# Values and keys of two tiles as seven block products, the norm's last sum on GpSimd, pages turned in place, and the second batch's pages fetched in front

## The chip, the cores and the metric

The kernel runs on one core of a Trainium2 chip. A core has five engines that work side by side, each with its own in-order queue of instructions: TensorE (PE in the profile; its weight loads are shown as PEld), VectorE (DVE), ScalarE (ACT), GpSimd (POOL) and SyncE (SP), which here does nothing but issue transfers. Sixteen DMA engines move data between HBM and the core's memory SBUF; TensorE writes to the small memory PSUM. An instruction waits on semaphores for what it needs, and everything behind it in the same queue waits too.

The metric is device time in microseconds (us) of one launch, as the median over several runs. A profiled execution is one more run, with every instruction recorded.

## What is computed

Sixty-four sequences of 32 rows by 512 columns go through four stages, each added to its input. Everything is in fp32. Cut to what matters:

```python
x = x + einsum('bct,bcd->bdt', x, W0[cond])             # stage 0: mix 32 rows
x = x + x @ base_w.T + bias + (x @ A.T) @ B.T            # stage 1: linear + LoRA
q, k, v = x @ Wq.T, x @ Wk.T, x @ Wv.T                   # stage 2: 32 query heads, 8 kv heads, D = 128
q, k = rope(rmsnorm(q, wq), pos), rope(rmsnorm(k, wk), pos)
k_all = concat(k_cache[block_table], k)                  # 16 pages of 32 keys, then 32 new ones
v_all = concat(v_cache[block_table], v)
probs = softmax(where(valid, q @ k_all.T * SCALE, -1e30))
x = x + (probs @ v_all) @ Wo.T
x = x + einsum('bct,bcd->bdt', x, W3[cond])              # stage 3: mix 32 rows
```

The norm is `t * rsqrt(mean(t*t) + eps) * w` over the 128 columns of a head. The rotation adds two products: the head times the cosines, and its halves exchanged times the sines.

## The kernel before

The 2048 rows are 16 tiles of 128 rows (four sequences each). Stages 0 and 1 run tile by tile (class `First`) at the front of the program and are also laid into the beginning of the attention. The attention dominates. It runs over two groups of 4 kv heads and, in each, over the 16 tiles: 32 steps. A step has four sequences, so there are 128 units, and each unit has four slots, one per kv head: 512 slots in all. One slot's scores are 128 queries (4 heads by 32 rows) against 512 cached and 32 new keys.

The order of instructions on the five engines is written by hand. A table `plan` holds, for each slot, lists of calls under names such as "fetch", "pe", "dve", "act" and "store"; `slot(i)` emits them: transfers, GpSimd's gathers, the scores of this slot (L827, L830), the transposes of an earlier one (L869), pieces of projection, pieces of the norm, head transposes (L745), the values of a still earlier one (L882), then VectorE's softmax (L835, L851, L853), takes of projections, and copies by ScalarE. `home` is the slot from which the offsets of a part are counted, and `begin` is the first slot, 43 before the first scores.

**Projections.** The steps go in pairs of tiles, 16 pairs, with a window of 32 slots each. The projections of a pair lie in the window ahead of its use. Values and keys of the two tiles are four `Plain` products: each is four matmuls over 128 of the 512 input columns (L579), into a PSUM tile `proj_ps` of 128 by 512 that has a single buffer, and ScalarE copies the result out (L589 values, L596 keys). Queries come as two `Block`s. A `Block` computes the two tiles' products with two head columns as one 2 by 2 block product with seven products instead of eight (Strassen's scheme in Winograd's form): seven products of two matmuls each (L646) of sums of x (`x_12`, `x_34`, stored by L514 and loaded by L562) and sums of weights (`block_sum`, L615); ScalarE takes the first, and VectorE adds the others into `raw` (L658).

**Norm.** A norm's squares are summed by ScalarE (L696, one instruction per head). VectorE scales the sum (L701), GpSimd raises it to the power -1/2 (L703, `rstd`), and VectorE does four pieces: `scale` (L708), `straight` (L715), `swapped` (L727, two instructions) and `sum` (L737). TensorE then turns the heads (L745) and ScalarE copies them out (L757). The pieces stand in a list, and each slot takes some if VectorE has few takes in it. There are 160 norms: four of queries and one of keys for each of 32 steps.

**Pages.** The cached keys are turned before use: 16 tiles of 4 pages per group. A page tile is loaded into `page_rows` (L253), turned by TensorE (L269), copied by ScalarE into a second tile `page_T` (L279), and stored to a scratch tensor (L289), beside a plain copy of the values (L285). In front there are four buffers of `page_rows` and two of `page_T`; for the second group there is one of each. Each unit then fetches its 16 pages of keys one by one from the scratch by page number (L783, `kT`, two buffers), in the first slot of the unit before it. The cached values come by gathers on GpSimd (L105, `v_sb`), and the mask of valid keys is `pen` (L798, GpSimd).

**Queues.** Nearly all other transfers are issued by SP, in the order of the program: x (L392), its store (L507), the turned x (L510), the sums (L514), rotary tables (L384), the pages, the pairs' loads (L562, L567), the new values (stored at L592, loaded by L805), `kT`, and the attention's output (L918). Weights of the second group and of the output, and the first outputs read back (L1110), are issued by GpSimd.

**Last stage.** The output projection and the second mix run pair by pair, also with seven products (L1293). For the first pair the weight sums `w_2`, `w_1`, `w_4` are built by VectorE (L1288) after the additions into `x3` (L1303), which wait for loads of x (L1337).

Of the kernel before, what the change touches and what calls it, by code (L numbers as in the profile page):

```python
# [51 lines left out]
NG = 2  # L52
# [25 lines left out]
def resid_kernel(  # L78
# [39 lines left out]
    ints_sb = const.tile([P, N_INT], I32, name="ints_sb")  # L118
    nc.sync.dma_start(out=ints_sb, in_=ints)
# [3 lines left out]


    same = const.tile([P, P], F32, name="same")
    nc.gpsimd.memset(same, 0.0)
    for j in range(NB):
        nc.gpsimd.memset(same[j * S : (j + 1) * S, j * S : (j + 1) * S], 1.0)
# [13 lines left out]
    def rows_of(pool, name, source, n, size, lanes, times=1.0, first=0.0, tag=None):  # L142

        i = pool.tile([P, n], I32, name=name, tag=tag or name)
        for c in range(0, n, 64):
            m = min(n - c, 64)
            f = small.tile([P, 64], F32, name=f"{name}_f", tag="rows_f", bufs=2)
            nc.vector.tensor_scalar(
                f[:, :m], source[:, c : c + m], float(size), lanes, ALU.mult, ALU.add
            )  # L150
            nc.vector.tensor_scalar(i[:, c : c + m], f[:, :m], times, first, ALU.mult, ALU.add)
        return i
# [4 lines left out]
    table = ints_sb[:, I_TABLE : I_TABLE + B * NC]  # L157
# [5 lines left out]
    def channel_diagonal(pool, table, t):  # L163
# [61 lines left out]
    with ExitStack() as l2:  # L225
# [20 lines left out]
        class Turn:  # L246


            def __init__(self, g, c, pool, bufs):
                self.g, self.c, self.pool, self.bufs = g, c, pool, bufs  # L250
                self.first = 2 * g * PAGES * PSIZE + c * P
                self.rows = pool.tile([P, 2, 2 * D], F32, name="page_rows", bufs=bufs[0])
# [22 lines left out]
            def keep(self):  # L275
                self.turned = self.pool.tile(
                    [P, 4, KG, PSIZE], F32, name="page_T", bufs=self.bufs[1]
# [108 lines left out]
        class First:  # L386


            def __init__(self, t):
                self.t = t  # L390
                self.x = first_pool.tile([P, HID], F32, name="x_sb", bufs=5)
# [13 lines left out]
            def diagonal(self):  # L405

                self.diag = first_pool.tile([P, NB, S], F32, name="mix_diag", bufs=2)
# [74 lines left out]
            def keep_out(self):  # L482
                p, i = divmod(self.t, 2)
                pool = first_pool if p else proj_pool
# [3 lines left out]
                if p == 0:  # L488
# [30 lines left out]
        def own_ranks(i):  # L519


            mask_i = first_pool.tile([P, P], I32, name=f"mask_i{i}")
# [3 lines left out]
            low = small.tile([P, P], F32, name="mask_low", bufs=1)  # L526
# [13 lines left out]
        class Pair:  # L540
# [13 lines left out]
            def load(self, name):  # L554
                src = {
                    "a": xT_dram[2 * self.p],
                    "b": xT_dram[2 * self.p + 1],
# [3 lines left out]
                self.x[name] = proj_pool.tile([P, NC, P], F32, name=f"x_{name}")  # L561
# [7 lines left out]
        class Plain:  # L569


            def __init__(self, pair, i, kind):
                self.pair, self.i, self.kind = pair_of[pair], i, kind
                self.step = self.pair.steps[i]

            def project(self, c):
                if c == 0:
                    self.ps = ps_m.tile([P, HID], F32, name="proj_ps", tag="m")
                nc.tensor.matmul(  # L579
                    self.ps,  # L580
                    lhsT=self.pair.x["ab"[self.i]][:, c, :],
                    rhs=w_sb[self.kind][:, c, :],
                    start=(c == 0),
                    stop=(c == NC - 1),
                )

            def take_values(self):
                self.v = proj_pool.tile([P, KG * D], F32, name="v_rows")
                nc.scalar.copy(self.v, self.ps)  # L589

            def store_values(self):
                nc.sync.dma_start(out=vn_dram[self.step.g][self.step.t], in_=self.v)  # L592

            def take_keys(self, norm):
                norm.raw = proj_pool.tile([P, REP, D], F32, name="raw", bufs=6)
                nc.scalar.copy(norm.raw, self.ps.rearrange("p (h d) -> p h d", h=REP))  # L596

        def block_sum(b, what):


            if (what, b) == (3, 0):
                for i, tag in ((2, 7), (1, 6), (4, 8)):
                    w_sb["sum", i] = None
            if what != 3 and w_sb["sum", what] is None:
                w_sb["sum", what] = wpool.tile(
                    [P, 2, NC // 2, REP * D], F32, name=f"sum{what}", tag=f"w{ {1: 6, 2: 7, 4: 8}[what]}"
                )
# [9 lines left out]
        def blocks(b):  # L617
            even, odd = w_sb["q", 2 * b], w_sb["q", 2 * b + 1]
            found = {"11": even[:, lo], "21": even[:, hi], "3": odd[:, lo], "22": odd[:, hi]}
            for i in (1, 2, 4):  # L620
                if w_sb["sum", i] is not None:
                    found[str(i)] = w_sb["sum", i][:, b]
            return found

        class Block:

# [15 lines left out]
            def project(self, i, c):  # L642
                x, half, w = self.ORDER[i]
                if c == 0:
# [3 lines left out]
                    lhsT=self.pair.x[x][:, half][:, c, :],  # L648
# [36 lines left out]

        class Norm:
# [5 lines left out]
            def squares(self):  # L692
                self.ss = small.tile([P, REP], F32, name="ss")
                sq = proj_pool.tile([P, REP, D], F32, name="sq", tag="sq", bufs=2)
                for h in range(REP):
                    nc.scalar.activation(  # L696
                        sq[:, h, :], self.raw[:, h, :], AF.Square, accum_out=self.ss[:, h : h + 1]
# [24 lines left out]
            def swapped(self):  # L722
                which = 3 if self.k is None else 1
                self.b = proj_pool.tile([P, REP, D], F32, name="rot_b", tag="sq", bufs=2)
# [11 lines left out]
            def sum(self):  # L736
                nc.vector.tensor_tensor(self.a, self.a, self.b, ALU.add)  # L737
# [24 lines left out]
        class Unit:  # L762


            def __init__(self, u):
# [7 lines left out]
                at = I_TABLE + b * NC  # L773
                for i in range(NPP // NC):
                    _, page = nc.values_load_multi_w_load_instructions(
                        ints_sb[i * S : i * S + 1, at : at + NC],
# [25 lines left out]
            def fetch_new(self):  # L802

                self.v_new = room["v"].tile([P, D], F32, name="v_new", bufs=3)
# [50 lines left out]
            def flip_new(self):  # L855
# [7 lines left out]
                self.pT_new = room["attn"].tile([P, P], F32, name="pT_new")  # L863
# [75 lines left out]
        def norm_piece(slot):  # L939
# [7 lines left out]
            if norm:  # L947
                slot += 1
# [519 lines left out]
```

## Time and profile before

| what | value |
|---|---|
| median of 3 runs | 2531.39 us (2530.64 to 2532.98) |
| the profiled execution | 2528.74 us |
| its span, first to last instruction | 2526.8 us |
| TensorE matmul busy | 2477.7 us, 98% |
| VectorE busy | 1659.7 us, 66% |
| ScalarE busy | 1281.1 us, 51% |
| GpSimd busy | 1098.3 us, 43% |
| `Plain` matmuls (L579), share of the chain | 9% |
| norm's last sum (L737) | 160 x 717 ns = 114.7 us of VectorE |
| gathers of values (L105) | 512 x 1025 ns = 525.0 us of GpSimd |

In the profile, `L646 PE MATMUL proj_ps<-sum,x 128x512` reads: line 646, engine, operation, what is written and what is read by the program's names, and the shape; `x224` is the number of instructions, and a fp32 matmul counts as two. Behind a bar stand the group's busy time in us, the mean ns of one, and the engine's idle time ahead of the group with what ended it. In an order of time, a line is the start in us, the duration in us, the engine and the instruction, and in square brackets the idle time before and its releaser. The chain of waits is followed back from the last instruction: a "DMA" piece is a transfer under way, an "SPq" piece an issue on SP's queue, an "issue" piece a time in which nothing shown was waited for.

### The profile page before, as it was taken

What the parts mean: (1) busy time and instruction counts of PE and PEld (TensorE: products, weight loads), DVE (VectorE), ACT (ScalarE), POOL (GpSimd) and SP (SyncE); (2) the same over time, 40 slices, a digit from 0 to 9 for tenths busy, and PEclk for the clock granted to TensorE, in tenths of its full rate; (3) what the DMA queues carried; (4) which work ended last, traced back from release to release, by engine and by line L of the source; (5) the groups of instructions that cost most, each with busy time, mean ns of one, the idle gap of its engine ahead of it and who ended that gap; (6) DMA issues with size and microseconds to landing.
All of it is one profiled execution on the core that took longest, in us unless ns stands there. A gap on an engine that the chain in (4) does not pass through costs nothing.

```text
span 2526.8 us, 46803 instructions
## 1 busy us (share of the span) xinstructions
PE 2477.7 (98%) x13824; PEld 1872.2 (74%) x13824; DVE 1659.7 (66%) x4154; ACT 1281.1 (51%) x3671; POOL 1098.3 (43%) x921
## 2 busy tenths in 40 slices
PE   7998999999999999999999999999999999999999
PEld 4555777777777777777777777777777777888887
DVE  5556767677767676787777776777776765433222
ACT  1335666666666666666666666666666644000000
POOL 4325545554545455654545455554555652000000
PEclk9999999999999999999999999999999999999999
DMA  6966666666666667866565656665656774233221
GB/s 225 308 211 195 183 194 190 192 188 191 193 183 196 192 203 216 262 182 195 174 193 164 192 171 181 174 187 167 186 174 214 234 258 157 101 111 127 98 84 59
DMA packets 442556, 461.50 MB, mean 183 GB/s; under 512 B 50560, under 2 KB 364800, under 8 KB 434496
## 3 DMA queue, kind: packets, MB, share of 16 engines
q1 hardware_dynamic: 393200, 296.21, 37.9%
q0 software_dynamic: 49104, 162.31, 21.2%
q8 instruction: 112, 1.84, 0.3%
q14 instruction: 140, 1.15, 0.1%
HBM read 387.02 MB, written 79.69 MB: 185 GB/s over the span
## 4 chain that ended last, share of the span: by engine, by line
PE 91%; DMA 3%; DVE 2%; issue 1%; SPq 1%; ACT 1%; POOL 1%; DVEq 0%; ACTq 0%; POOLq 0%
PE o_ps L882 17%; PE proj_ps L646 14%; PE out_ps L1293 14%; PE s_ps L827 10%; PE proj_ps L579 9%; PE s_ps L830 8%; PE pT_ps L869 8%; PE head_ps L745 3%; PE l_ps L471 2%; PE o_ps L894 2%; DMA kT<-kT 1%; DMA v_sb<-v,v_rows 1%; DMA v_new<-vn 1%; DVE rot_a L737 1%; PE mix_ps L1311 1%
## 5 line engine op out<-in xcount | busy, mean ns | idle before, releaser
L105 POOL DMA_INDIRECT v_sb<-v,v_rows x512 | 525.0, 1025 | 458.4 <-PE o_ps L882 358.7
L835 DVE CUSTOM_DVE_ANT_0 sm<-s_ps,pen 128x544 f32<-128x544 f32 x512 | 370.8, 724 | 453.0 <-PE s_ps L830 447.4
L882 PEld LDWEIGHTS o_ps<-pT,v_sb 128*128 128x128 f32 x4096 | 520.8, 192 | 141.0 <-issue 134.5
L846 ACT ACTIVATE sm<-sm,top 128x544 f32<-128x544 f32 x512 | 382.5, 747 | 460.1 <-DVE top L835 460.0
L882 PE MATMUL o_ps<-pT,v_sb 128*128 128x128 f32 x4096 | 542.2, 275 | 4.1 <-DMA v_sb<-v,v_rows 4.0
L852 ACT ACTIVATE sm<-sm,share 128x512 f32<-128x512 f32 x512 | 369.9, 722 | 181.1 <-DVE share L851 178.1
L703 POOL TENSOR_TENSOR rstd<-ss,minus_half 128x4 f32<-128x4 f32 x160 | 191.8, 1199 | 469.1 <-DVE ss L701 464.2
L827 PE MATMUL s_ps<-kT,qT 128*128 128x288 f32 x1024 | 348.1, 422 | 7.1 <-DMA kT<-kT 4.4
L871 DVE COPY pT<-pT_ps 128x512 f32<-128x512 f32 x512 | 351.1, 686 | 1.6 <-PE pT_ps L869 1.5
L869 PE MATMUL pT_ps<-ident,sm 128*128 128x128 f32 x2048 | 307.7, 273 | 0.0
L830 PE MATMUL s_ps<-kT,qT 128*128 128x256 f32 x1024 | 305.1, 380 | 1.7 <-issue 1.7
L869 PEld LDWEIGHTS pT_ps<-ident,sm 128*128 128x128 f32 x2048 | 256.3, 141 | 51.5 <-issue 0.2
L798 POOL TENSOR_SCALAR pen<-key_f,seq_f 128x544 f32<-128x544 f32 x128 | 279.6, 2184 | 15.9 <-DMA x_b<-xT 5.1
L830 PEld LDWEIGHTS s_ps<-kT,qT 128*128 128x128 f32 x1024 | 194.8, 190 | 56.1 <-issue 2.1
L696 ACT ACTIVATE sq<-raw 128x128 f32<-128x128 f32 x640 | 189.9, 298 | 35.4 <-DVE raw L658 32.0
L105 POOL DMA_INDIRECT mix_rows<-in_w,cond_rows x32 | 34.5, 1077 | 324.2 <-DVE mix_diag L168 307.6
L1342 ACT COPY p<-out_ps 128x256 f32<-128x256 f32 x7 | 2.6, 372 | 340.2 <-PE out_ps L1293 340.2
L1293 PE MATMUL out_ps<-w,o_in 128*128 128x256 f32 x768 | 170.0, 384 | 4.1 <-DVE w L1288 4.1
L827 PEld LDWEIGHTS s_ps<-kT,qT 128*128 128x128 f32 x1024 | 155.1, 191 | 24.3 <-issue 5.0
L1293 PEld LDWEIGHTS out_ps<-w,o_in 128*128 128x128 f32 x768 | 147.8, 193 | 25.1 <-DVE w L1288 4.5
L853 DVE TENSOR_SCALAR p_new<-sm,share 128x32 f32<-128x32 f32 x512 | 148.5, 290 | 18.2
L1293 PE MATMUL out_ps<-wo,o_in 128*128 128x256 f32 x704 | 155.6, 379 | 0.8 <-ACT oT L911 0.8
(160 smaller groups left out, 3442.7 us busy)
## 6 DMA issues: line engine op xcount, KB each, us to landing
kT<-kT SPq DMA_DIRECT2D x2048, 64.0 KB
o<-oT SPq DMA_DIRECT2D x29, 1024.0 KB
o_in<-o SPq DMA_DIRECT2D x28, 1024.0 KB
rot<-rot SPq DMA_DIRECT2D x48, 256.0 KB
page_rows<-in_kv_cache SPq DMA_DIRECT2D x32, 256.0 KB
vn<-v_rows SPq DMA_DIRECT2D x32, 256.0 KB
v<-in_kv_cache SPq DMA_DIRECT2D x32, 256.0 KB
kT<-page_T SPq DMA_DIRECT2D x32, 256.0 KB
```

The lines of the kernel that those rows point to most:

```text
L105: nc.gpsimd.indirect_dma_start(out=dst, out_offset=None, in_=table, in_offset=bass.IndirectOffsetOnAxis(ap=index, axis=0),)
L646: nc.tensor.matmul(self.ps, lhsT=self.pair.x[x][:, half][:, c, :], rhs=blocks(self.b)[w][:, c, :], start=(c == 0), stop=(c == 1),)
L798: nc.gpsimd.tensor_scalar(self.pen, key_f, seq_f[:, self.b : self.b + 1], BIG, ALU.is_ge, ALU.mult)
L827: nc.tensor.matmul(ps[:, first:HID], lhsT=q, rhs=self.kT[:, :n1, k, :], start=True, stop=True)
L830: nc.tensor.matmul(ps[:, HID : first + LA], lhsT=q, rhs=self.kT[:, n1:, k, :], start=True, stop=True)
L835: nc.vector.tensor_tensor_reduce(out=sm, in0=ps[:, first : first + LA], in1=self.pen, scale=1.0, scalar=3e38, op0=ALU.add, op1=ALU.min, ac ...
L846: nc.scalar.activation(sm, sm, AF.Exp, bias=top, scale=-1.0, accum_out=total)
L852: nc.scalar.activation(sm[:, :L], sm[:, :L], AF.Copy, scale=share)
L869: nc.tensor.transpose(ps[:, c, :], self.sm[k][:, c * P : (c + 1) * P], ident)
L871: nc.vector.tensor_copy(pT, ps)
L882: nc.tensor.matmul(self.o_ps[k], lhsT=self.v[c][:, k * D : (k + 1) * D], rhs=self.pT[k][:, c, :], start=(c == 0), stop=False,)
L1293: nc.tensor.matmul(ps[:, :HALF], lhsT=o[:, i, :], rhs=w[i // REP][:, i % REP, :], start=(i == 0), stop=(i == KG * REP - 1),)
```

## The change

1. `Plain` is gone. Values and keys of a pair's two tiles are one more `Block`, `KV`, with seven products of two matmuls. Its even weights are the values', its odd ones the keys', and its weight sums have tiles of their own, built by four more additions per group. ScalarE takes the first product and VectorE the other six. The values are stored from `raw`. Of `x_b` only the half that a `Block` reads is loaded, for the first pair too. The weights of values and keys are loaded earlier in front, and their sums are built there. The slots of the query products move by up to one.
2. The norm's last `sum` is issued on GpSimd as soon as `swapped` is issued on VectorE; the turn of the heads comes at least two slots later, not one. The squares of the heads of a norm are written to one tile of one head's size.
3. Pages are turned in place: ScalarE's copy goes back to `page_rows`. In front the load comes two slots ahead, not three; the second group has one buffer.
4. x tiles have four buffers, not five, and are loaded three slots ahead of `home`, not five. The 16 key pages of unit 1 are fetched in slot -4, not 0.
5. The second group's weights and the output's weights are loaded at other slots. The first pair's early products in the last stage are kept in the weight pool, `w_2` is combined ahead of the additions into `x3`, and the pattern `same` is built anew for the last stage. Integer tables are split into two tiles, and `v_new` and `pT_new` have a buffer less each.

The diff, cut to its core:

```diff
@@ class Turn
-                self.rows = pool.tile([P, 2, 2 * D], F32, name="page_rows", bufs=bufs[0])
+                self.rows = pool.tile([P, 2, 2 * D], F32, name="page_rows", bufs=bufs)
...
-                self.turned = self.pool.tile(
-                    [P, 4, KG, PSIZE], F32, name="page_T", bufs=self.bufs[1]
+                self.turned = self.rows.rearrange("d i f -> d (i f)").rearrange(
+                    "d (p k s) -> d p k s", p=4, k=KG
                 )
@@ class First
-                self.x = first_pool.tile([P, HID], F32, name="x_sb", bufs=5)
+
+            def load(self):
+                t = self.t
+                self.x = first_pool.tile([P, HID], F32, name="x_sb", bufs=4)
                 nc.sync.dma_start(out=self.x, in_=x[t * P : (t + 1) * P, :])
@@ class Pair
-                    "b": xT_dram[2 * self.p + 1],
+                    "b": xT_dram[2 * self.p + 1][:, hi],
@@ def blocks(b)
-            even, odd = w_sb["q", 2 * b], w_sb["q", 2 * b + 1]
+            even, odd = (w_sb[1], w_sb[0]) if b == KV else (w_sb["q", 2 * b], w_sb["q", 2 * b + 1])
@@ class Block
+            def store_values(self, norm, i):
+                step = self.pair.steps[i]
+                nc.sync.dma_start(
+                    out=vn_dram[step.g][step.t], in_=norm.raw.rearrange("p h d -> p (h d)")
+                )
@@ class Norm
-                sq = proj_pool.tile([P, REP, D], F32, name="sq", tag="sq", bufs=2)
+                sq = proj_pool.tile([P, D], F32, name="sq")
...
-                nc.vector.tensor_tensor(self.a, self.a, self.b, ALU.add)
+                nc.gpsimd.tensor_tensor(self.a, self.a, self.b, ALU.add)
@@ def norm_piece(slot)
             piece()
             if norm:
-                slot += 1
+                norm.sum()
+                slot += 2
                 while slot in turning or (slot - VLAG) % KG == KG - 1:
                     slot += 1
@@ def begin_block(pair, b, slots)
-                    norm = Norm(pair, i // 5, 2 * b + (i in (4, 5)))
-                    at(last, "pe", begin_norm, last, norm)
+                    if b != KV:
+                        norm = Norm(pair, i // 5, 2 * b + (i in (4, 5)))
+                    else:
+                        norm = Norm(pair, i // 5)
+                    if b == KV and i in (1, 6):
+                        at(last, "store", block.store_values, norm, i // 5)
+                    else:
+                        at(last, "pe", begin_norm, last, norm)
@@ the plan of the pairs
-            for kind, j, slots in (
-                (1, 0, (0, 0, 1, 2)),
-                (1, 1, (3, 3, 4, 5)),
-                (0, 0, (6, 6, 7, 8)),
-                (0, 1, (9, 9, 10, 10)),
-            ):
...
-                    (11, 11, 12, 13, 14, 14, 15, 16, 17, 17, 18, 19, 20, 20),
-                    (21, 22, 23, 23, 24, 25, 26, 26, 27, 28, 29, 29, 30, 31),
+            for b, slots in (
+                (KV, (0, 0, 1, 2, 3, 3, 4, 5, 6, 6, 7, 8, 9, 9)),
+                (0, (10, 11, 12, 12, 13, 14, 15, 15, 16, 17, 18, 18, 19, 20)),
+                (1, (21, 21, 22, 23, 24, 24, 25, 26, 27, 27, 28, 29, 30, 30)),
...
+                for w, what in zip((-1, 0, 2, 5) if g == 0 else (-12, -11, -10, -9), (3, 2, 1, 4)):
+                    at(home + w, "dve", block_sum, KV, what)
...
-                places = [6, 11, 21, 23, 32, 34] + ([27, 25] if g == NG - 1 else [36, 38])
+                places = (6, 11, 16, 21, 29, 34, 31, 27) if g == NG - 1 else (3, 9, 14, 21, 25, 32)
@@ the plan of the tiles, pages and units
-            at(home - 5 if t > 1 else begin, "fetch", make, *f, First, t)
+            at(home - 3 if t > 1 else begin, "fetch", call, *f, "load")
...
-            at(home - 6, "fetch", lambda t: make(turn_of, t, Turn, 1, t, room["pages"], (1, 1)), t)
+            at(home - 6, "fetch", lambda t: make(turn_of, t, Turn, 1, t, room["pages"], 1), t)
...
-            at(home - 3 if c > 3 else begin + 8, "fetch", make, turn_of, key, Turn, 0, c, start_pool, (4, 2))
+            at(home - 2 if c > 3 else begin + 8, "fetch", make, turn_of, key, Turn, 0, c, start_pool, 4)
...
-            at(KG * (u - 1) if u else ready, "fetch", make, unit_of, u, Unit, u)
+            at(KG * (u - 1) if u > 1 else ready + 2 * u, "fetch", make, unit_of, u, Unit, u)
@@ the program's front
-                at(begin + 6, "store", load_kv_weights, 0, 1, j)
-                at(begin + 8, "store", load_kv_weights, 0, 0, j)
+                at(begin + 3, "store", load_kv_weights, 0, 1, j)
+                at(begin + 4, "store", load_kv_weights, 0, 0, j)
@@ the last stage, first pair
                     p1 = early["p1"]
+                    w_1, w_2, w_4 = new_block("w_1"), new_block("w_2"), new_block("w_4")
+                    combine(w_2, w_3, w11, ALU.add)
                 for at_last in waiting:
                     mixed(*at_last)
...
-                    w_1, w_2, w_4 = new_block("w_1"), new_block("w_2"), new_block("w_4")
-                    combine(w_2, w_3, w11, ALU.add)
```

## The prediction

> **What bounds the kernel now.** I read the page's busy shares and chain first, then windows of the span, then groups of instructions and the order of time at the places that the diff touches. From the page:
>
> ```profile
> PE 2477.7 (98%) x13824; PEld 1872.2 (74%) x13824; DVE 1659.7 (66%) x4154; ACT 1281.1 (51%) x3671; POOL 1098.3 (43%) x921
> ...
> PE 91%; DMA 3%; DVE 2%; issue 1%; SPq 1%; ACT 1%; POOL 1%; DVEq 0%; ACTq 0%; POOLq 0%
> ...
> L835 DVE CUSTOM_DVE_ANT_0 sm<-s_ps,pen 128x544 f32<-128x544 f32 x512 | 370.8, 724 | 453.0 <-PE s_ps L830 447.4
> ```
>
> TensorE is the bound. The last line shows VectorE's slack: once in most of the 512 slots it waits for the scores, 447.4 us / 437 waits = 1.02 us each. Windows (PE, PEld, DVE, ACT, POOL, clock, DMA share, GB/s) show where TensorE is not alone:
>
> ```profile
> 60.00:90.00 30.00, 26.83 (x111) 15.23 (x109) 15.46 (x38) 5.95 (x12) 8.59 (x7) 1.00 0.91 307
> ...
> 400.00:1000.00 600.00, 599.64 (x3555) 447.85 (x3554) 438.34 (x1156) 383.59 (x1106) 309.87 (x251) 1.00 0.66 194
> ...
> 2000.00:2200.00 200.00, 188.39 (x1117) 160.77 (x1116) 124.66 (x271) 75.75 (x188) 71.43 (x67) 0.97 0.58 188
> ```
>
> In the steady part work taken from TensorE should come off one for one. Around 60 to 150 us the DMA is nearly full; at the ends there are stalls.
>
> **Matmuls removed.** Values and keys of a pair of tiles were 4 x 4 matmuls, and become 7 x 2: two fewer for each of 16 pairs. Their price, from the order of time in the steady part:
>
> ```profile
> 1003.19 1.88 PE L646 MATMUL proj_ps<-sum,x_b 128*128 128x512 f32 x4
> ...
> 1007.15 1.02 PE L646 MATMUL proj_ps<-wq,x_a 128*128 128x512 f32 x2
> ...
> 1008.02 1.05 PE L882 MATMUL o_ps<-pT,v_sb 128*128 128x128 f32 x8
> ```
>
> One matmul is two instructions, and from 1007.15 to the next work at 1008.02 it holds TensorE 0.87 us (the four from 1003.19 to 1004.91 give 0.86 each). 30 x 0.86 = 25.8 us for the 15 pairs in the steady part; 1.7 us for the first pair, which stands in the front part and may be covered (0 to 1.7; I take 1). Together -26.8.
>
> **Takes, sums and the norm's last sum.** The groups:
>
> ```profile
> L658 DVE TENSOR_TENSOR raw<-proj_ps,raw 128x512 f32<-128x512 f32 x224 | 150.4, 683 | 7.0 <-PE proj_ps L646 7.0
> ...
> L737 DVE TENSOR_TENSOR rot_a<-rot_a,rot_b 128x512 f32<-128x512 f32 x160 | 114.7, 717 | 0.1
> ...
> L429 POOL TENSOR_TENSOR x_sb<-x_sb,bias_sb 128x512 f32<-128x512 f32 x16 | 20.3, 1270 | 26.8 <-PE x1T_ps L434 21.5 <-DVE v_rows_f L148 4.7 <-PE h_ps L455 0.5
> ```
>
> VectorE gains 7 more accumulating takes per pair (112 x 0.683 = 76.5 us) and 8 weight sums (1.22 us each by the row at 77.97 us in the front part: 9.8), and loses 160 x 0.717 = 114.7: 28 us lighter. ScalarE loses 4 copies and gains 1 per pair: 48 x 0.578 (the copy of L589) = 28 us lighter. GpSimd gains 160 sums. The nearest row is L429's sum of the same shape, 1.27 us: 203 us, 1098 + 203 = 1301 of 2527. None of the three becomes the bound; 64 us more in 600 puts GpSimd at about 62%.
>
> What can leak onto TensorE: (a) the single projection bank: each product's first matmul waits for the take before. In before the waits on VectorE's takes come to 0.5 + 2.3 + 1.5 = 4.3 us for 32 blocks, 0.13 each; 16 more give 2 us, from which ScalarE's takes go (1.2 + 3.7 us, most of that once, in the front part). (b) GpSimd works in order: a sum waits for VectorE's `swapped`, and the gathers of values, the mask `pen` and the next `power` stand behind it. (c) A sum on GpSimd can hold VectorE. Both are seen in the front part:
>
> ```profile
> 76.81 1.28 POOL L429 TENSOR_TENSOR x_sb<-x_sb,bias_sb 128x512 f32<-128x512 f32 x1
> ...
> 83.01 1.27 POOL L429 TENSOR_TENSOR x_sb<-x_sb,bias_sb 128x512 f32<-128x512 f32 x1 [3.00 <-PE x1T_ps L434]
> ```
>
> ```profile
> 77.36 0.69 DVE L426 TENSOR_TENSOR x_sb<-mix_ps,x_sb 128x512 f32<-128x512 f32 x1 [0.57 <-PE mix_ps L417]
> ...
> 83.15 1.27 DVE L373 TENSOR_TENSOR rot<-trig,q_cos 128x128 f32<-128x128 f32 x1 [2.96 <-DMA rot<-rot]
> 84.35 0.28 DVE L373 TENSOR_TENSOR rot<-trig,q_sin 128x128 f32<-128x128 f32 x1
> ```
>
> Beside the sum of 83.01 an SBUF-only 0.28 us operation takes 1.27 and ends with it; beside that of 76.81 an operation with one input in PSUM keeps its 0.69. In a slot the sum follows the slot's last piece; what VectorE does next is L835, the copy of pT and the takes, all reading PSUM, and its 1.02 us pause. So I take little: 0.02 us per sum, 3 us for (b) and (c), 2 for (a) less 1; bounds 0 and 160 x (1.27 - 1.02) = 40 us, the block beyond the mean slack. Steady leak +4. The turn of a head comes a slot later and is due slots ahead: 0.
>
> The Trainium skill ("GPSIMD Engine Reference", section 3.1 Elementwise and section 4.1 Engine selection) speaks against this move: an elementwise operation with two inputs goes to VectorE, GpSimd taking 1.96 times as long; this trace's rows give 1270 / 717 = 1.77. By the page 160 x 0.717 x 1.96 = 225 us on GpSimd, an estimate, in place of 203; either fits beside TensorE, so the sum is the same by both.
>
> **Pages turned in place (front part).** The copy goes back into the page's own buffer; ScalarE no longer waits for the store of two pages before, but the load of page c+4, on SP, waits for the store of page c, issued just ahead of it. Today (order of time, the chain):
>
> ```profile
> 84.39 4.93 DMA kT<-page_T
> ...
> 90.55 3.23 PE proj_ps L579 x4
> ```
>
> Behind the first lies TensorE's one long stall of 60 to 150 us, 3.7 us before 90.55: it goes. In its place SP stands for about 4.9 us (stores there land after 4.1 to 6.6) in each of slots -25 to -14, and behind it are queued the x loads, whose SP wait on the store of x is already 31.6 us in 11 times. By adding up SP's issues and waits I get a two-slot cycle of 10.8 to 13.4 us against TensorE's 10.7: 0 to 2.6 us for 6 cycles, 0 to 15. Loads are issued about 9 us ahead of use and eat part of it: I take +4, less 3.7 = 0 (bounds -3.7 to +12). The x loads two slots before use instead of four share this bound. The half-size x_b load, and the earlier KV weights at 15 to 30 us where TensorE idles anyway, count 0 (0 to 3: 1 MB at 360 GB/s).
>
> **The next keys fetched in front.** The 16 page loads of unit 1 move from slot 0 to slot -4, past x of pair 1, its sums' stores and x_b on SP:
>
> ```profile
> 180.51 9.39 SPq L783 DMA_DIRECT2D kT<-kT  x16
> ...
> 192.64 1.15 SPq L514 DMA_DIRECT2D xS<-x  x2
> 193.89 0.42 SPq L562 DMA_DIRECT2D x_b<-xT  x1
> 198.85 0.65 SPq L805 DMA_DIRECT2D v_new<-vn  x1
> 200.51 10.98 SPq L783 DMA_DIRECT2D kT<-kT  x16
> ```
>
> ```profile
> 199.15 2.12 POOL L798 TENSOR_SCALAR pen<-key_f,seq_f 128x544 f32<-128x544 f32 x1 [5.13 <-DMA x_b<-xT]
> ...
> 208.81 4.03 DMA v_sb<-v,v_rows
> ```
>
> Today the chain runs from the xS store (lands 198.5) over the first mask, the gathers, a second mask, to the values at 212.89, then 1.72 us for unit 1's last keys at 213.93. Afterwards the last of these goes (-1.7), and xS and x_b are issued up to 9.4 us later, unless that queue is early; one or two sums of 1.27 us stand among the gathers. 9.4 + 1.3 - 1.7 = +9; bounds -1.7 and +11; I take +7, as part of those 9.4 us is TensorE work still to do.
>
> **The last stage.** `w_2` is combined ahead of the x3 additions. Today VectorE waits for x there, and TensorE with it:
>
> ```profile
> 2142.31 2.96 DMA x<-x
> ...
> 2145.89 1.15 DVE w L1288
> ```
>
> TensorE is ready at 2143.0 and starts at 2147.08, 4.07 us on L1288. The new order needs only the weights and the space: -4 (bounds -4.1, 0). Other weights' places, 2 or 3 slots earlier or later on GpSimd's queue: 0, within the 6 us that TensorE idles in 2030 to 2065 (bounds -3, +3).
>
> **Sum:** -26.8 + 4 + 0 + 7 - 4 = -19.8. The profiled execution took 2528.74 us (span 2526.8), 2.65 below the median 2531.39 of the runs (2530.64 to 2532.98). 2528.74 - 19.8 = 2509; the median would be 2512, which I predict. Own range: 2502 to 2523.
>
> **Rivals.**
> 1. Everything added is hidden: -26.8 - 4 - 3.7 - 1.7 = -36, at the median 2495 to 2502. For it: slack on three engines. Against: SP's order at 180 to 200 us is a queue, not an average.
> 2. The front part eats the gain: +12 and +11 in place of 0 and +7, and no gain at L1288: -26.8 + 4 + 12 + 11 = 0, 2526 to 2536. For it: DMA at 0.91 to 0.96, SP's waits. Against: it needs every bound at once.
> 3. Slower: the sum on GpSimd holds VectorE or the gathers on the path of the scores. Price 0.25 us of TensorE for each of 160 sums (1.27 less the slack 1.02): 40 us in place of 3: 2512 + 37 = 2549. It decides above (20 + 5 + 3) / 160 = 0.17 us each. For it: 83.15 above. Against: 77.36, and that VectorE loses 0.72 us in the same slot.
> 4. The products not falling by two per pair is excluded by the edit's slots: 14 in place of 16.
>
> **How the numbers follow.** Forecast 0.62, rival 1 0.13, rival 2 0.09, rival 3 0.16. A measurement of this kernel can tell 0.2%, 5.1 us, from no change: faster is under 2526.3, slower over 2536.5. Faster takes the forecast, rival 1 and a little of rival 2: 0.77; same the rest: 0.07; slower 0.16. The range leaves out rival 3 and some of rival 1: 2497 to 2536.
>
> **What would show it.** PE busy about 2450 with the share still 98% in 400 to 1600 us; L646 with 48 x 14 x 2 = 1344 instructions; under L737 160 GpSimd sums of about 1.27 us; waits of TensorE for L658 about 6 us; the first values at about 220 us less what the front gained; no 4 us before the first L1293 of the last stage. I am wrong if idle TensorE time in 400 to 1600 grows past 10 us, if pT copies or L835 lengthen beside L737, or if the first values come later than 225 us.

## The result, and the profile after

The changed kernel is slower: 2539.12 us in the median of 20 runs (2533.35 to 2547.70) against 2529.49 us of the kernel before in 20 runs beside it; ratio 1.0041, 95% interval 1.0031 to 1.0051. The forecast, 2512 in a range of 2497 to 2536, was wrong in its sign. The profiled executions differ by 2535.6 - 2526.8 = 8.8 us of span.

Busy shares and chain of the changed kernel:

```profile
PE 2464.5 (97%) x13760; PEld 1861.5 (73%) x13760; DVE 1717.2 (68%) x4114; ACT 1305.9 (52%) x3623; POOL 1303.7 (51%) x1086
...
PE 88%; DVE 5%; DMA 4%; SPq 1%; issue 1%; ACT 0%; POOL 0%; ACTq 0%; DVEq 0%; POOLq 0%
```

The 64 instructions less on TensorE (32 matmuls) are there, but its share fell from 98 to 97% and VectorE's on the chain rose from 2 to 5%. VectorE should have become 28 us lighter; it is 57 us busier. The windows of the changed kernel (busy time of PE, PEld, DVE, ACT, POOL, clock, DMA share, GB/s) show that TensorE now stands idle where it did not, 6.7 us in 400 to 1000 against 0.4, and 8.5 us in 1000 to 1600:

```profile
400.00:1000.00 600.00, 593.34 (x3531) 444.38 (x3530) 452.72 (x1141) 393.83 (x1106) 373.58 (x302) 1.00 0.66 195
1000.00:1600.00 600.00, 591.53 (x3505) 440.38 (x3504) 466.52 (x1153) 388.50 (x1091) 378.97 (x304) 1.00 0.63 188
```

To see where the time went I laid the two traces beside each other at marks that both have: the taking of a tile's first mix (VectorE's `x_sb<-mix_ps`), the start of each of the 512 softmaxes on VectorE (`sm`, one per slot), and the first product of the last stage. Times are us; "forecast" is what the prediction's steps come to in that stretch.

| stretch | before | changed | difference | forecast |
|---|---|---|---|---|
| start to the 8th tile's mix | 77.4 | 78.1 | +0.7 | -1 to 0 |
| 8th to 16th mix (pages turned) | 89.8 | 96.3 | +6.4 | 0 |
| 16th mix to the first softmax | 34.1 | 45.3 | +11.2 | +7 |
| slots 0 to 192 | 729.6 | 722.4 | -7.2 | -10.3 + its part of 4 |
| slots 192 to 256 (change of group) | 244.5 | 253.9 | +9.4 | -3.4 |
| slots 256 to 464 | 784.6 | 780.4 | -4.2 | -11.2 + its part of 4 |
| slot 464 to the last stage | 175.8 | 175.0 | -0.8 | -0.9 |
| last stage | 391.0 | 384.2 | -6.8 | -4 |
| sum | 2526.8 | 2535.6 | +8.7 | -19.8 |

Every column is one execution, and the stretches do not repeat equally well. Slots 256 to 464 took 780.4 us in each of the four kernels that have this part as the changed kernel has it (after, e3, e4, g3 below). Elsewhere stretches that no edit touches differ by several us from trace to trace: in the changed kernel and the experiments the first one took 78.1 to 80.9 us, slot 464 to the last stage 169.6 to 178.3.

A part of the difference is TensorE's granted clock. It is 1.0 in most of the span, with short stretches at 0.5. The longest begins while TensorE waits for the first softmax and lasts 6 us into the slots:

```profile
212.80:226.50 13.70, 5.62 (x10) 3.20 (x11) 6.26 (x13) 4.84 (x8) 8.17 (x6) 0.50 0.43 137
```

Scores that take 0.65 us later (L817) take 1.33 us there. An estimate of what it costs is half of TensorE's busy time at 0.5: 2.8 us here, none at this place in the kernel before. Over the whole trace TensorE was busy for 24.8 us at 0.5 in the changed kernel and for 15.2 us in the kernel before, by the same estimate some 5 of the 8.8 us. What brings the clock down was not tested.

The losses have places. Three of them can be read straight from the changed kernel's trace.

First, the mask of unit 0. The chain of waits runs over SP's 32 issues of key pages, then the store of the sums; the order of time of SP and of GpSimd there:

```profile
190.53 9.37 SPq L773 DMA_DIRECT2D kT<-kT  x16
...
201.80 9.34 SPq L773 DMA_DIRECT2D kT<-kT  x16
...
212.19 0.37 SPq L570 DMA_DIRECT2D x_b<-xT  x1
212.96 0.85 SPq L521 DMA_DIRECT2D xS<-x  x2
```

```profile
217.48 2.12 POOL L788 TENSOR_SCALAR pen<-key_f,seq_f 128x544 f32<-128x544 f32 x1 [10.99 <-DMA xS<-x]
```

The second row of 16 used to come behind the sums. Now the first mask waits for them (it started at 199.15 before), the first softmax reads the mask at 219.63, and TensorE waits 12.64 us for that softmax.

Second, one stall that comes back in every window of 32 slots. Order of time of VectorE, GpSimd and TensorE in the changed kernel, in a part where only attention and projections run:

```profile
1388.26 0.75 DVE L717 TENSOR_TENSOR rot_b<-raw,rot 128x256 f32<-128x256 f32 x2
...
1389.11 1.35 DVE L843 TENSOR_SCALAR p_new<-sm,share 128x32 f32<-128x32 f32 x1
1389.16 1.26 POOL L727 TENSOR_TENSOR rot_a<-rot_a,rot_b 128x512 f32<-128x512 f32 x1 [1.77 <-DVE share L841]
...
1390.38 0.68 DVE L642 TENSOR_TENSOR raw<-proj_ps,raw 128x512 f32<-128x512 f32 x1
...
1391.11 1.98 PE L630 MATMUL proj_ps<-wq,x_a 128*128 128x512 f32 x4 [0.60 <-DVE raw L642]
...
1392.93 1.05 PE L872 MATMUL o_ps<-pT,v_sb 128*128 128x128 f32 x8
```

`p_new`, 128 by 32 values and mostly 0.24 us, begins 0.05 us ahead of the norm's sum on GpSimd and ends with it, 1.35 us later. The take behind it is late, and TensorE waits for the single projection bank: 0.60 us, and from the start of its four instructions to the next work at 1392.93 it is then 1.82 us, not the 1.72 of four without a wait. The wait comes back in slot 20 of every window. In the whole trace 62 of 512 `p_new` take over 0.8 us, every one of them beside a sum, and none does in the kernel before (longest 0.72 us):

```profile
L843 DVE TENSOR_SCALAR p_new<-sm,share 128x32 f32<-128x32 f32 x512 | 209.7, 410 | 18.1
```

Third, SP in front. The waits on SP's queue of the changed kernel, 0 to 225 us (total, times, longest):

```profile
SPq L256 <- DMA kT<-page_rows: 29.9, 11, 5.0
SPq L399 <- DMA x<-x_sb: 25.0, 11, 5.6
```

and what it does to the queue (the last two lines are from TensorE's order of time):

```profile
109.42 0.65 SPq L293 DMA_DIRECT2D kT<-page_rows  x1
```

```profile
117.20 0.63 PE L272 MATMUL s_ps<-ident,page_rows 128*128 128x128 f32 x4 [0.85 <-DMA page_rows<-in_kv_cache]
122.86 1.10 PE L424 MATMUL mix_ps<-x_sb,mix_diag 128*128 128x512 f32 x2 [1.98 <-DMA x_sb<-in_x]
```

The store issued at 109.42 lands 4.40 us after its issue by the chain; only then is the next page loaded, and x behind it. In the kernel before TensorE waited for neither a page nor an x tile between 100 and 200 us.

### The profile page after: what moved, and what is told of

It is laid out like the page before. It is cut to its first block, busy times and chain, and to the rows that moved or that the text cites. A ratio compares the mean times of both kernels' runs of the same rounds, so it can differ in the third digit from the quotient of the medians.

```text
span 2535.6 us, 46991 instructions
## 1 busy us (share of the span) xinstructions
PE 2464.5 (97%) x13760; PEld 1861.5 (73%) x13760; DVE 1717.2 (68%) x4114; ACT 1305.9 (52%) x3623; POOL 1303.7 (51%) x1086
## 4 chain that ended last, share of the span: by engine, by line
PE 88%; DVE 5%; DMA 4%; SPq 1%; issue 1%; ACT 0%; POOL 0%; ACTq 0%; DVEq 0%; POOLq 0%
PE proj_ps L630 21%; PE o_ps L872 17%; PE out_ps L1274 14%; PE s_ps L817 10%; PE s_ps L820 8%; PE pT_ps L859 8%; PE head_ps L735 3%; PE o_ps L884 2%; PE l_ps L478 2%; DVE p_new L843 1%; DMA kT<-page_rows 1%; DVE sm L825 1%; DMA v_sb<-v,v_rows 1%; DMA x_sb<-in_x 1%; PE s_ps L852 1%
## 5 line engine op out<-in xcount | busy, mean ns | idle before, releaser
L872 PEld LDWEIGHTS o_ps<-pT,v_sb 128*128 128x128 f32 x4096 | 520.4, 192 | 135.2 <-issue 124.1
L693 POOL TENSOR_TENSOR rstd<-ss,minus_half 128x4 f32<-128x4 f32 x160 | 198.5, 1241 | 368.0 <-DVE ss L691 365.5
L817 PE MATMUL s_ps<-kT,qT 128*128 128x288 f32 x1024 | 350.6, 424 | 13.7 <-DVE top L825 13.4
L727 POOL TENSOR_TENSOR rot_a<-rot_a,rot_b 128x512 f32<-128x512 f32 x160 | 205.6, 1285 | 197.2 <-DVE share L841 148.5
L686 ACT ACTIVATE sq<-raw 128x128 f32<-128x128 f32 x640 | 198.1, 309 | 82.2 <-DVE raw L642 52.3
L642 DVE TENSOR_TENSOR raw<-proj_ps,raw 128x512 f32<-128x512 f32 x336 | 225.4, 682 | 8.4 <-PE proj_ps L630 6.0
L843 DVE TENSOR_SCALAR p_new<-sm,share 128x32 f32<-128x32 f32 x512 | 209.7, 410 | 18.1
L630 PE MATMUL proj_ps<-sum,x 128*128 128x512 f32 x384 | 192.1, 603 | 1.9 <-DVE raw L642 1.9
L817 PEld LDWEIGHTS s_ps<-kT,qT 128*128 128x128 f32 x1024 | 155.6, 192 | 33.2 <-DVE top L825 15.9
```

What stands on the lines that cost most here:

```text
L630: nc.tensor.matmul(self.ps, lhsT=self.pair.x[x][:, c if x == "b" else half.start + c, :], rhs=blocks(self.b)[w][:, c, :], start=(c == 0), ...
L817: nc.tensor.matmul(ps[:, first:HID], lhsT=q, rhs=self.kT[:, :n1, k, :], start=True, stop=True)
L872: nc.tensor.matmul(self.o_ps[k], lhsT=self.v[c][:, k * D : (k + 1) * D], rhs=self.pT[k][:, c, :], start=(c == 0), stop=False,)
```

## The experiments

The experiments ran in four groups (e, f, g and h), each on one chip with the kernel before beside it; ratios are to that, and a gain on the changed kernel is a difference of two such ratios. "Slots" are stretches as in the table above, each from one trace.

**e1: the norm's sum back on VectorE.**

```diff
-                nc.gpsimd.tensor_tensor(self.a, self.a, self.b, ALU.add)
+                nc.vector.tensor_tensor(self.a, self.a, self.b, ALU.add)
...
-                norm.sum()
-                slot += 2
+                slot += 1
...
-            for piece in (norm.scale, norm.straight, norm.swapped):
-                pieces.append((slot + 2, piece, norm if piece == norm.swapped else None))
+            for piece in (norm.scale, norm.straight, norm.swapped, norm.sum):
+                pieces.append((slot + 2, piece, norm if piece == norm.sum else None))
```

> The changed kernel with the norm's last sum back on VectorE, as a fourth piece of the list, and the turn one slot later as before. In the changed kernel the slots 256 to 464 take 780.4 us (before: 784.6; two matmuls less in each window of 32 slots would give 773.4), and once per window a GpSimd sum stretches p_new from 0.24 to 1.35 us just ahead of a take that TensorE waits for. Theory A (the sum on GpSimd holds VectorE's p_new): slots 256 to 464 take 773 to 776 us, p_new is back at 0.29 us on average, the time falls by 10 to 16 us. Theory B (the six takes on VectorE in place of ScalarE's are the cost, with one projection bank): 780 to 786 us and no gain, as VectorE gets 115 us more work.

Ratio 0.9993 (0.9982 to 1.0003): 12 us less than the changed kernel by the two ratios. Slots 256 to 464 took 774.4 us, `p_new` 0.283 us on average. Theory A; B falls: more work on VectorE (busy 1730.7 us against 1717.2), and less time.

**e2: the sum on GpSimd, but never released ahead of a slot's takes.**

```diff
-        def norm_piece(slot):
+        def norm_piece(slot, early=False):
...
+            if early and pieces[0][2]:
+                return
...
             run(i, "power")
-            norm_piece(i)
+            norm_piece(i, True)
```

> The changed kernel with the sum on GpSimd, but the piece that releases it (swapped) is never given to VectorE ahead of p_new and the takes of a slot, only behind them. Theory A: p_new falls from 0.41 us on average to under 0.33 and slots 256 to 464 take 773 to 777 us; the time falls by 8 to 14 us. Theory C (GpSimd's in-order queue is what is late: gathers behind the sum): p_new doesn't matter, slots 256 to 464 stay at 779 to 782 us.

Ratio 0.9989 (0.9978 to 1.0000), 13 us less than the changed kernel (20 us in the two traces, where TensorE was busy at the clock of 0.5 for 10.4 us against 24.8); slots 256 to 464 took 772.4 us, and over the whole kernel:

```profile
L843 DVE TENSOR_SCALAR p_new<-sm,share 128x32 f32<-128x32 f32 x512 | 143.2, 280 | 18.0
```

No `p_new` is over 0.8 us any more, with the sums still on GpSimd at 1.30 us each, and VectorE is busy for 1658.9 us in place of 1717.2. Theory A again; C falls, since the gathers still stand behind the sums. But e2 also moved `swapped` behind the takes, so one thing was left to separate.

**g2: `p_new` on ScalarE, nothing else.**

```diff
-                nc.vector.tensor_scalar(self.new[:, k, :], sm[:, L:], share, None, ALU.mult)
+                nc.scalar.activation(self.new[:, k, :], sm[:, L:], AF.Copy, scale=share)
```

> The changed kernel with p_new (128x32, in SBUF) done by ScalarE as a copy with a scale, and nothing else: swapped still stands ahead of the takes on VectorE, the sum stays on GpSimd. It tells apart the two things that e2 changed at once. Theory A (p_new stretched by the sum is what delays the take): slots 256 to 464 take 772 to 775 us (changed kernel 780.4, e2 772.4) and the time falls by 8 to 13 us. Rival O (it was swapped standing ahead of the take): 778 to 781 us, gain under 3 us.

Ratio 0.9933 (0.9916 to 0.9949), some 27 us less than the changed kernel by the two ratios (21 us in the spans of the traces), and slots 256 to 464 took 769.2 us: more than theory A expected, which was 8 to 13 us and 772 to 775. `swapped` and the sum are where they were. TensorE's waits for the takes show it; first the changed kernel, then g2 (matmuls with the weights of queries and the first tile's x):

```profile
L630 PE MATMUL proj_ps<-wq,x_a 128*128 128x512 f32 x256 | 127.6, 600 | 10.5 <-DVE raw L642 10.5
```

```profile
L630 PE MATMUL proj_ps<-wq,x_a 128*128 128x512 f32 x256 | 126.1, 595 | 0.6 <-DVE raw L642 0.6
```

Rival O falls. The gain goes 3 us beyond e2 in these slots: `p_new` was VectorE time ahead of the takes in the kernel before too, and there it was already lengthened now and then. 79 of its 512 took 0.3 to 0.72 us in that trace, 72 of them beside the mask `pen` on GpSimd. g2 takes both away; how much each is worth was not tried.

**e3: unit 1's key pages back in slot 0.**

```diff
-            at(KG * (u - 1) if u > 1 else ready + 2 * u, "fetch", make, unit_of, u, Unit, u)
+            at(KG * (u - 1) if u else ready, "fetch", make, unit_of, u, Unit, u)
```

> The changed kernel with the 16 key pages of unit 1 fetched in slot 0 again, not in slot -4. Theory D (these 16 issues on SP put the sums' store and x_b, and so the first mask, 11 us later): the first softmax starts at 208 to 212 us, not at 219.6, and the time falls by 8 to 11 us. Rival E (the wait only moves to the keys of unit 1): slot 8 comes less than 4 us earlier than in the changed kernel (248.4 us), and the time falls by under 4.

Ratio 1.0014 (1.0004 to 1.0023), 7 us less than the changed kernel, a little under what I had expected. The first softmax starts at 211.4 us, and from the 16th mix to it there are 36.3 us, 9.0 fewer; slot 8 comes at 239.9, 8.5 us earlier. Theory D; the wait doesn't move to unit 1's keys.

**e4: the second group's weight sums spread.**

```diff
-                for w, what in zip((-1, 0, 2, 5) if g == 0 else (-12, -11, -10, -9), (3, 2, 1, 4)):
+                for w, what in zip((-1, 0, 2, 5) if g == 0 else (-13, -10, -7, -4), (3, 2, 1, 4)):
```

> The changed kernel with the second group's four weight sums for values and keys in slots -13, -10, -7 and -4 of the next window in place of -12 to -9. Theory F (four sums of 1.2 us in successive slots that also hold takes overfill VectorE): between slots 208 and 220 the kernel loses under 1.5 us on the kernel before, in place of 3.6, the time falls by 2 to 4 us. Rival G (the loss there is the sum on GpSimd holding VectorE, or the waits for key pages at slot 200 that shift it): the loss stays at 3 us or more.

Ratio 1.0037 (1.0024 to 1.0049), against 1.0041: a loss on the kernel before of 1.2 us between slots 208 and 220 in place of 3.6, as F has it, but no gain that the times can tell. What stood there in the changed kernel, VectorE's order of time:

```profile
1021.32 1.35 DVE L843 TENSOR_SCALAR p_new<-sm,share 128x32 f32<-128x32 f32 x1
1022.59 1.21 DVE L597 TENSOR_TENSOR wk<-wk 128x1024 f32<-128x1024 f32 x1
1023.73 0.68 DVE L642 TENSOR_TENSOR raw<-proj_ps,raw 128x512 f32<-128x512 f32 x1
```

A stretched `p_new` and a weight sum stand one behind the other ahead of a take; TensorE waits 1.74 us at 1024.46. Both causes meet here.

**f1: e2, e3 and e4 at once.**

> The changed kernel with the three edits e2, e3 and e4 at once. If the three losses are separate, their gains on the changed kernel add: 13 (e2) + 7 (e3) + 1 to 3 (e4) = 21 to 23 us, so 11 to 14 us under the kernel before, ratio 0.9945 to 0.9958. Rival H (they share a wait, one filling what another frees): 13 to 16 us on the changed kernel, ratio 0.998 to 0.999.

Ratio 0.9938 (0.9923 to 0.9954): 26 us less than the changed kernel, at least the sum of the three. Rival H falls; the three losses are separate. One thing I had not expected: from the 8th to the 16th mix f1, f3 and f4 took 99.9 to 101.3 us, where e1 to e4 took 94.6 to 97.1, though none of the edits touches that stretch knowingly. SP's waits for the stores of keys are longer there, 36.3 to 36.9 us in place of 32.7 to 33.3. The f runs had another chip than the e runs; whether the chip or an edit does it stays open.

**f2: f1 with a fifth buffer for the pages in front.**

```diff
-            at(home - 2 if c > 3 else begin + 8, "fetch", make, turn_of, key, Turn, 0, c, start_pool, 4)
+            at(home - 2 if c > 4 else begin + 8, "fetch", make, turn_of, key, Turn, 0, c, start_pool, 5)
```

> f1 with a fifth buffer of page_rows in front, so that SP's load of a page waits for the store of five pages before, issued one slot earlier. From the eighth tile's mix to the sixteenth's the kernel before takes 89.8 us, the changed one and e1 to e4 94.6 to 97.1. Theory I (SP's wait for the store issued just ahead, 29.9 us in 11 waits, is what lengthens the front): 89 to 92 us, and 3 to 6 us less time than f1. Rival J (the x loads, two slots ahead of use in place of four, are what is late): 94 to 97 us as before, no gain on f1.

Ratio 0.9894 (0.9878 to 0.9909): 11 us less than f1, about twice what I had expected. The stretch takes 84.0 us, 5.8 less than in the kernel before. SP no longer waits for a store of keys in front at all, while its wait for the store of x, 25.0 us in the changed kernel, has grown (the first line of SP's waits, 0 to 225 us):

```profile
SPq L399 <- DMA x<-x_sb: 32.8, 12, 4.7
```

So theory I; J falls, as the x loads were left where the change had put them.

**g3: the changed kernel with the fifth buffer alone.**

> The changed kernel with the fifth page buffer in front and nothing else. Theory I (the store's wait on SP): from the eighth mix to the sixteenth 84 to 87 us (changed kernel 96.3), and the time falls by 8 to 12 us, near the kernel before. Rival P (the front is late by several causes and the buffer alone frees only one): 92 us or more, gain under 5 us.

Ratio 0.9988 (0.9978 to 0.9997), 13 us less than the changed kernel; the stretch takes 84.0 us again. Theory I; P falls. A single buffer of 2 KB per partition undoes more than the whole loss.

**f3: f1 with the second group's weights loaded where the kernel before loads them.**

```diff
-                places = (6, 11, 16, 21, 29, 34, 31, 27) if g == NG - 1 else (3, 9, 14, 21, 25, 32)
+                places = (6, 11, 16, 21, 29, 34, 31, 27) if g == NG - 1 else (6, 11, 21, 23, 32, 34)
```

> f1 with the second group's weights loaded at the old offsets (6, 11, 21, 23, 32, 34) in place of (3, 9, 14, 21, 25, 32). In slots 199 to 208 the changed kernel and e1 to e4 lose 2 to 5 us on the kernel before, where TensorE waits for key pages and values. Theory K (the weights' 2 MB come while the keys of the next units are fetched, and which slots they take decides): within 1 us of the kernel before in slots 199 to 208. Rival L (chance of the transfers): 2 to 5 us lost here too.

Slots 199 to 208 took 33.6 us (kernel before 34.2, f1 38.5), as theory K has it; but slots 224 to 256 took 124.0 in place of 121.4, and the ratio, 0.9937 (0.9921 to 0.9953), is f1's. The waits for weights and pages move with the places; half of the gain is given back.

**g1: f2 with f3's places.**

> f2 (the three edits and a fifth page buffer) with the weights' places of f3. f3 took slots 199 to 208 back to 33.6 us (f1: 38.5, f2: 40.0) but gave 2.4 us of it back by slot 240 and was no faster than f1 by the medians. If that holds, the time is that of f2 within 2 us, ratio 0.9885 to 0.9900; if the places are a gain of their own, 4 to 6 us under f2, ratio 0.987 to 0.988.

Ratio 0.9872 (0.9855 to 0.9889): by the ratios 5.6 us under f2, as the second expectation has it, by the profiled spans 1.3 us (2498.6 us, f2's 2499.9, on another chip), as the first has it. Slots 199 to 208 are at 33.6 us, slots 224 to 256 at 124.1. The intervals of f2 and g1 overlap, so this settles nothing more.

**f4: f1 with `w_2` combined late again.**

```diff
                     p1 = early["p1"]
-                    w_1, w_2, w_4 = new_block("w_1"), new_block("w_2"), new_block("w_4")
-                    combine(w_2, w_3, w11, ALU.add)
...
                     p_2, p_7 = early["p2"], early["p7"]
+                    w_1, w_2, w_4 = new_block("w_1"), new_block("w_2"), new_block("w_4")
+                    combine(w_2, w_3, w11, ALU.add)
```

> f1 with w_2 combined behind the additions into x3 again, as in the kernel before. The last stage, from its first product to the end, takes 391.0 us in the kernel before and 384.2 in the changed one. Theory M (all of it is the earlier w_2): 389 to 391 us, and 4 to 7 us more time than f1. Rival N (it is something else, the early weights or the queues): 384 to 386 us.

Ratio 0.9956 (0.9940 to 0.9972), 4.5 us more than f1; the last stage takes 389.1 us, and TensorE stands again, now for 2.75 us:

```profile
2132.38 7.99 PE L1276 MATMUL out_ps<-w,o_in 128*128 128x256 f32 x28 [2.75 <-DVE w L1271]
```

Theory M for 4.9 of the 6.8 us. The other 1.9 are in the traces: f4 has 0.8 us less idle time of TensorE in this stage than the kernel before (7.1 and 7.9), and a shorter stretch at the clock of 0.5 behind the stall, 3.4 us against 5.7 us of busy time in the kernel before:

```profile
2146.00:2152.80 6.80, 5.72 (x14) 4.55 (x15) 6.80 (x7) 0.00 (x0) 0.00 (x0) 0.50 0.67 261
```

Half of the difference is 1.1 us, an estimate. The changed kernel has no such stretch in this stage.

**h1: all of it, with `p_new` on ScalarE in place of e2's edit** (g2, e3, e4, f2's buffer and f3's places on the changed kernel).

> The changed kernel with p_new on ScalarE, unit 1's key pages back in slot 0, the four weight sums spread, a fifth page buffer and the old weights' places (g1 with g2's edit in place of e2's). g2 took slots 256 to 464 in 769.2 us where g1 took 772.3; over the 464 slots behind the front that would be 6 to 7 us: 2491 to 2494 us, ratio 0.984 to 0.987. If it was only the second group that gained, 3 us: 2495 to 2497.

Ratio 0.9858 (0.9841 to 0.9874), inside what I expected: 2486.4 us against 2522.7 beside it, 36 us less than the kernel before. Window of its steady part:

```profile
400.00:1000.00 600.00, 600.00 (x3603) 451.70 (x3602) 403.10 (x1005) 429.67 (x1288) 383.78 (x309) 1.00 0.66 198
```

TensorE has no idle time left in it, with the sum on GpSimd and 14 products per pair.

## Why the prediction was wrong

**Matmuls removed (-26.8): right.** Where nothing stands against it the saving is there: slots 256 to 464 are 6.5 windows, 6.5 x 1.72 = 11.2 us, and e2 took 12.2 us less than the kernel before in them, with the seven products in place.

**Steady leak (+4): the step that failed most.** It came to 13 us by the ratios of e2. The trace of before had shown the effect, the 0.28 us rotary operation at 83.15 that took 1.27 us beside a sum on GpSimd. I then asked what VectorE does after a slot's last piece, and answered with operations that read PSUM. That is true of the late pieces. But the first of the three places for pieces in `slot` lies ahead of `divide`, so `swapped` can end, and the sum begin, right at `p_new`, which reads and writes only SBUF and stands ahead of a take. I priced 0.02 us per sum against a mean slack of 1.02 us per slot. Measured: of 11.2 us due in slots 256 to 464, all at a clock of 1.0, only 4.2 came: 7.0 us lost in 6.5 windows of ten sums, 0.11 us per sum on the mean, in truth 1.1 us per window, most of it the one stall of slot 20. (Of 10.3 us due in slots 0 to 192 there came 7.2, but there the clock behind the first softmax accounts for about 2.8 of the 3.1.) TensorE's waits for VectorE's takes came to 19.6 us in 24, against some 6 forecast. The mean slack hides nothing if the one operation that is stretched is followed by the one that TensorE waits for.

**No engine becomes the bound: right, and not enough; the change of group was put at nothing.** I added up VectorE's work over the program. At the change of group eight sums of weights for queries and four new ones of 1.2 us meet takes that ScalarE used to do, and the early weights meet the key pages. The prediction had nothing there; the stretch cost 9.4 us where -3.4 was due. e4 shows 2.4 us for the four sums in a row, f3 that the weights' places move a wait of 4.9 us of which half comes back; e1 and e2 took 248.9 and 248.6 us there in place of 253.9, so the stretched `p_new` has its part too, and some 1.7 of the 9.4 us are the clock (3.4 us busy at 0.5, from 974.0 us on). With all the remedies of h1 the stretch takes 242.9 us, within 2 us of what was due; how the rest of the loss divides among them stays open.

**Pages in place (0, bounds -3.7 to +12): right mechanism, wrong size.** +6.4 in the changed kernel. I had priced SP's wait at about 4.9 us in each of 12 slots; it was 29.9 us in 11 times, 2.7 each, so what was mis-sized is how much the early loads absorb. I had worked out a cycle of 10.8 to 13.4 us for two slots, and let loads issued 9 us ahead absorb most of it. With loads two slots ahead and four buffers little is absorbed, since a wait on SP delays all loads behind it. g3 shows that with one more buffer the wait and the whole loss are gone. The other half of the step was right: ScalarE's wait for `page_T` is gone, and with a fifth buffer the stretch is 5.8 us shorter than before.

**Key pages in front (+7): right, the size low.** +11.2, just over the upper bound; I had let TensorE's remaining work cover part of the 9.4 us, and it covered next to none: TensorE's idle time in this stretch grew from 6.4 to 15.7 us. e3 takes back 9.0 of the 11.2 in its trace and 7 us by the ratios.

**Last stage (-4): right**, by f4 (4.9); 1.9 more came in these two traces, about 1.1 of it by the clock.

**The signs.** Of the three signs of being wrong that the prediction names two came: TensorE's idle time in 400 to 1600 us was 15.1 us, over the 10, and the first values began at 231.41 us, after 225. The third did not: the copies of pT and the softmaxes kept their times, because the operation that was held was one I had not listed.

**The rivals.** None came alone. Rival 2 needed every bound at once, and I held that against it; its two front terms did come (17.6 of 23 us). Rival 3's price of 40 us was too high, but its mechanism took 13 us by e2, 0.08 us per sum, half of the 0.17 at which it would have decided alone. Causes that each fall short of the turning point went over it together.

## What to carry to other kernels

An operation's slack has to be read at the operation that stands behind it in its queue, not as a mean over the slot: list what the moved work can run beside, and what waits for that. When a buffer is reused in place, the wait moves to whoever fills it next; if that is an in-order transfer queue, everything behind pays, and one more buffer can be worth more than what was saved. Losses in separate places can add up, as e2, e3 and e4 do in f1, so a forecast should also weigh the case in which several middling bounds come together.

## What the runs showed of the hardware

An operation on VectorE that reads and writes only SBUF can be held for as long as a two-input sum on GpSimd runs: `p_new` took 1.35 us beside a sum of 1.26, 62 times in the changed kernel, and mostly 0.24 us otherwise. It went by the order: 102 `p_new` overlap a sum, and the 40 that began 0.06 us or more ahead of it kept their 0.24 to 0.25 us (as at 435.76, with its sum at 435.82), while the 62 that began later, from 0.05 us ahead on, all ended 0.04 us behind it. Not every such operation is held: in e2 the reciprocal `share`, of one column, took 0.16 us as always in two places where it ran wholly within a sum (917.29 and 1998.94). Operations with an input in PSUM were not lengthened: the copy of pT has a mean of 686 ns before and 685 ns with 160 sums on GpSimd, the takes 683 and 682. The Trainium skill ("GPSIMD Engine Reference", section 1. Specifications) says that GpSimd shares its SBUF interfaces with VectorE and contends with instructions in a two-port mode or with two inputs in SBUF; the runs agree that they contend. The rotary operation at 83.15 has two inputs in SBUF; `p_new` has one and a column of factors, and in which mode it runs the trace does not show.

A stop of TensorE costs a little more than the idle time shown: after 0.60 us of idle time at 1391.11 the next four instructions held it for 1.82 us in place of 1.72, and so they did at all 16 stops ahead of four such instructions between 250 and 2050 us. That is 0.10 us on top of the wait.

At a granted clock of 0.5 matmuls take about twice as long: the two of L817 took 1.33 us at 220.41, and 0.65 us at 232.41, where the clock is 1.0 again.
